# Two attention blocks on one core: the layer-1 score convolution moved behind the projection and split in halves twice

## The chip, the cores and the metric

The kernel runs on one core of one Trainium2 chip. The metric is the device time of one execution in microseconds (us), the lower the better. A core has TensorE (matrix products, PE in the profile), VectorE (DVE), ScalarE (ACT), GpSimd (POOL) and SyncE (SP, which here issues DMAs). Everything is computed in 32-bit floating point.

## The reference, cut to what matters

The input is `x` with 8 images of 512 channels and 32 x 32 = 1024 positions. Two layers follow each other. Both normalise in groups of channels, make queries, keys and values by a 512 x 512 product over the channels, apply attention over the 1024 positions, project, and add the input.

```python
# layer 0: 32 groups, 8 heads of 64 channels
h = group_norm(x, gn_weight, gn_bias)
q, k, v = split(einsum('oc,bct->bot', w_qkv, h) + b_qkv)
weight = softmax(einsum('bct,bcs->bts', q * scale, k * scale))
a = einsum('bts,bcs->bct', weight, v)
x = x + einsum('oc,bct->bot', w_proj, a) + b_proj
# layer 1: 8 groups, one head of 512 channels
xn = group_norm(x, gamma, beta)
q, k, v = conv1x1(xn, q_w, q_b), conv1x1(xn, k_w, k_b), conv1x1(xn, v_w, v_b)
attn = softmax(einsum('bqc,bck->bqk', q, k) * scale)
x = x + conv1x1(einsum('bqk,bkc->bqc', attn, v), p_w, p_b)
```

## The kernel before, in words

**Fused weights.** In layer 1 the query and key weights are multiplied into one matrix `m` in the prologue, and value and output weights into `z`. So layer 1 needs one convolution `g` (with `m`), the scores of `g` against `h`, a product `z` by token, and the weighted sum of `z`.

**Products by halves (`wino`).** A 512-wide product is split in halves on both sides and computed with 7 half-size products in place of 8, in the scheme of Strassen and Winograd. It needs sums and differences of the halves of both factors ("factors"): `left_sums` and `right_sums` list them as steps, and `image_factors` and `weight_factors` hold them. The weights' factors are made once and kept in DRAM (`keep`). `wino` runs the products in the order 1, four in `middle`, then 4 and 3. One product is a step: 4 matmuls of 128x512 (two output halves `i`, two slices `k` of the sum). Its results pass through three pairs of accumulator banks, a, b and c. ScalarE copies bank a (`t`), VectorE adds (`u`, `w`, and the outputs in `done`). The last two steps (4 and 3) are put on `tail` and issued inside the next product, after its step 1, so that TensorE has other work while the banks are read.

**Halves twice (`conv2`).** The convolutions k and q of layer 0, from the second image on, apply the scheme twice: 49 matmuls of 128x256 in four "pairs" of outer products. The inner factors of the image are made on GpSimd (`inner_factors`), those of the weights in the prologue (`keep2`, GpSimd), and the weights come in two parts.

**Background and hooks.** `background` is a list of small pieces of VectorE or GpSimd work; each step of a product issues a few of them (`back`). `all_background` issues what is left. `hooks` are calls after given steps of a product. What is issued with `keep_in_program_order` keeps its place in its engine's queue; the rest is ordered by a scheduler when the program is built. All TensorE work is kept in program order.

**The order of one image b** (b from 1): attention of layer 0 (`attention0`), g of layer 1 for image b-1 with the projection p of image b begun in its tail, p with the residual and the group-norm statistics (`projection`), layer 1's scores for b-1 in two parts (`scores1`), z, the weighted sum (`values1`), then v of image b+1 and its k and q. So layer 1 lags one image behind. For image 0 there is no layer 1 yet: v of image 1, then p, then k and q. After the last image layer 1 of the last image runs alone.

**Attention of layer 0.** Eight blocks, four pairs of heads `hp` by two halves of the positions `tb`. In each, 8 pairs of score matmuls, ScalarE's exponentials, VectorE's 7 additions into `sum`, 8 pairs of `av` matmuls, the `sums` matmuls with ones, VectorE's reciprocal, and a trip through DRAM (`rows`, then `r`) which spreads the reciprocals over the partitions; GpSimd (for the last block VectorE, `scaled`) multiplies `a` by `r`. `extra` lists pieces of work after the score matmuls and after the av matmuls of each block.

**Group norm.** `half_stats` and `end_stats` are VectorE's bn_stats and aggregate. `group_mean` is a small matmul `gmean` over the channels, and VectorE's copy, `d`, `d2`, `dv`. `affine` is the matmul `gvar` on `dv`, and scale and offset. In the kernel before, `norm_hooks` places the flush of the background, gmean and gvar in part 0 of the scores, after its third, fourth and fifth step.

**Weights** are loaded by `load_weight` in the order of `uses` into three buffers.

Of the kernel before, what the change touches and what calls it, by code (L numbers as in the profile page):

```python
# [29 lines left out]
def two_attention_blocks_kernel(  # L30
# [145 lines left out]
    def main_path(ctx):  # L176
# [117 lines left out]
        wdram2 = {n: dram.tile([P, 7, 7, P], F32, name=f"sums2_{n}") for n in "qk"}  # L294

        def keep2(n, t):

            u = wpool.tile([P, 4, 7, P], F32, tag="w", name=f"prepare2_{n}")
            quarter = lambda k, i: t[:, :, k, ts(i, P)]
            a11, a21, a12, a22 = quarter(0, 0), quarter(0, 1), quarter(1, 0), quarter(1, 1)  # L300
            s1, s2, s3, s4 = (u[:, i, :, :] for i in range(4))
            for dst, x, y, op in (
                (s1, a21, a22, ALU.add), (s2, s1, a11, ALU.subtract), (s3, a11, a21, ALU.subtract),
                (s4, a12, s2, ALU.subtract),
            ):
                nc.gpsimd.tensor_tensor(dst, x, y, op)
            for j, f in enumerate((a11, a12, s4, a22, s1, s2, s3)):
                nc.sync.dma_start(wdram2[n][:, :, j, :], f)

        twice = [("k", 0), ("k", 1), ("q", 0), ("q", 1)]  # L310
        uses = ["v", "p", *twice] if B > 1 else ["p"]
        for b in range(1, B):
            uses += ["m", "p", "z"] + (["v", *twice] if b + 1 < B else [])
# [3 lines left out]
        def load_weight():  # L317
            if uses:
                n = uses.pop(0)
                t = wpool.tile([P, 7 * C], F32, tag="w", name=f"w_{n[0]}_{len(uses)}")  # L320
                if n in twice:
                    t = t.rearrange("p (i j m) -> p i j m", i=4, j=7)
                    i = n[1]
                    t = t[:, : 4 - i]
                    nc.sync.dma_start(t, wdram2[n[0]][:, 4 * i : 4 + 3 * i])
                else:
                    t = t.rearrange("p (i k m) -> p i k m", i=7, k=2)
                    nc.sync.dma_start(t, wdram[n])
                loaded.append((n, t))
# [10 lines left out]
        def image_factors(h, uid):  # L340

            tiles = [pair_tile(f"t{i}_{uid}") for i in (1, 2, 4)]
            halves = lambda t: (t[:, :HT], t[:, HT:])
            return right_sums(
                [halves(t) for t in h[:2]], [halves(t) for t in h[2:]],
                [lambda j, t=t: t[:, j, :] for t in tiles], nc.vector.tensor_sub,
            )
# [52 lines left out]
        def inner_factors(hf, uid):  # L400

            f, steps = {}, []
            for p in ORDER:
                t = big_tile(f"inner{p}_{uid}", (P, 4, 2 * P))
                t1, t2, t3, t4 = (t[:, i, :] for i in range(4))
                b11, b12, b21, b22 = (hf[p][k][:, ts(i, 2 * P)] for k in range(2) for i in range(2))
                f[p] = {1: b11, 2: b21, 3: b22, 4: t4, 5: t1, 6: t2, 7: t3}

                def make(ops=((t1, b12, b11), (t2, b22, t1), (t3, b22, b12), (t4, b21, t2))):
                    for dst, x, y in ops:  # L410
                        nc.gpsimd.tensor_tensor(dst, x, y, ALU.subtract)

                steps.append(make)
            return f, steps

        def conv2(n, f, bias, name, hooks=(), late=None):
# [123 lines left out]
            last = [lambda: biased_half(0, 1), lambda: biased_half(1, 0)]  # L540
# [3 lines left out]
            pair(3, (3, 4), [(0, 1), (1, 0)], [(0, 1), (1, 0)], [load_weight, *last])  # L544
# [3 lines left out]
        def reciprocals(total, uid, across):  # L548
# [14 lines left out]
            nc.sync.dma_start(rows.rearrange("j i n -> i j n"), rc[0:P:32, :, :])  # L563
            if across:
                r = pair_tile(f"r_{uid}")
                for j in range(2):
                    row = rows[j : j + 1].rearrange("j i n -> j (i n)")
                    nc.sync.dma_start(r[:, j, :], row.to_broadcast([P, HT]))
            else:
                r = rpool.tile([P, HT], F32, tag="r", name=f"r_{uid}")  # L570
                for j in range(2):
                    row = rows[j : j + 1].rearrange("j i n -> j (i n)")
                    nc.sync.dma_start(r[ts(j, 64), :], row.to_broadcast([64, HT]))
# [3 lines left out]
        def attention0(b, q, k, v, extra):  # L577
            a = channel_tiles(f"a0_{b}")
            n = 0
            for hp in range(KC):  # L580
                for tb in range(2):
# [31 lines left out]
                    r = reciprocals(total, uid, False)  # L613
                    if (hp, tb) != (KC - 1, 1):
                        nc.gpsimd.tensor_tensor(dst, dst, r, ALU.mult)  # L615
                    else:
                        scaled = lambda dst=dst, r=r: nc.vector.tensor_mul(dst, dst, r)

            assert not extra
            return a, scaled  # L620


        def scores1(b, gf, hf, uid, hooks):
# [7 lines left out]
            def part(j):  # L631
# [34 lines left out]
                wino(f"sc_{uid}_{j}", mm, done, middle=(6, 2, 5, 7) if j else (2, 5, 6, 7), hooks=() if j else hooks)  # L666
# [85 lines left out]
        def prologue():  # L752
# [35 lines left out]
            k = conv(weight_factors(first["k"][0]), hf, pcols("bk0"), "k0_0")  # L788
            finish()
            keep2("k", first["k"][0])  # L790
            norm1.group_mean(acc_tile("gmean_0_1")[:, :KC])
# [6 lines left out]
            for n in "pmz":  # L798
                t, steps = prepare(n)
                later.append(steps)  # L800
                later.append([lambda n=n, t=t: keep(n, t), load_weight])
# [3 lines left out]
                lambda: tc.keep_in_program_order(nc.vector.tensor_add(obias[0], bias[2], pcols("bp0"))),  # L805
            ])
# [27 lines left out]
        def attention_steps(a, scaled, b):  # L834
            af, steps = image_factors(a, f"a_{b}")
            return af, [[], [scaled, lambda: background.extend(steps)]]

        def projection(b, af, xt):

            norm = GroupNorm(1, f"1_{b}")  # L840

            def residual(i, r, c, ps, u):
                oc = 2 * r + i
                xh = xt[oc][:, ts(c, HT)]
                nc.vector.scalar_tensor_tensor(xh, ps, obias[0][:, oc : oc + 1], xh, ALU.add, ALU.add)
                if u is not None:
                    nc.vector.tensor_add(xh, xh, u)  # L847
                background.append(lambda: norm.half_stats(oc, c, xh))

                if c == 1 - r:  # L850
                    background.append(lambda: norm.end_stats(oc))
# [6 lines left out]
            by_channel(weight("p"), af, f"p_{b}", residual, after=[load_weight, store])  # L858
            return norm

        def norm_hooks(norm, uid):
            return [
                [], [], [all_background], [lambda: norm.group_mean(acc_tile(f"gmean_{uid}")[:, :KC])],
# [3 lines left out]
        def values(b, h, hooks=()):  # L867

            hf, steps = image_factors(h, f"h0_{b}")
            background.extend(steps)  # L870
# [21 lines left out]
        def layer1_scores(b, h, hooks):  # L892
            hf, steps = image_factors(h, f"h1_{b}")
            background.extend(steps)
            g = conv(
                weight("m"), hf, ubias, f"g1_{b}", middle=(2, 5, 6, 7), hooks=hooks, back=4,
                after=[load_weight, lambda: background.extend(gsteps)],
            )
# [6 lines left out]
            return hf, gf  # L905

        def layer1_rest(b, hf, gf, hooks, ahead):
            e, total, ef = scores1(b, gf, hf, f"1_{b}", hooks)
# [19 lines left out]
        for b in range(B):  # L928
# [11 lines left out]
            for i, f in enumerate(applies):  # L940
                extra[2 * i + 3].append(f)
            if b > 0:
                extra[0] += late
            psum_pools(f"attention_{b}", 1)
            a, scaled = attention0(b, q, k, v, extra)
            psum_pools(f"products_{b}", 2)
            xt = [load_x(b, c, "x") for c in range(KC)]
            af, ends = attention_steps(a, scaled, b)
            if b > 0:
                hf, gf = layer1_scores(b - 1, h, ends)  # L950
                norm1 = projection(b, af, xt)
# [5 lines left out]
                layer1_rest(b - 1, hf, gf, norm_hooks(norm1, f"1_{b}"), ahead)  # L957
                if b + 1 < B:
                    v, f, norm0 = values(b + 1, h)
                    q, k, late = keys_and_queries(b + 1, f, norm0, ())  # L960
            elif B > 1:
                v, f, norm0 = values(1, h, ends)
                norm1 = projection(0, af, xt)
                q, k, late = keys_and_queries(1, f, norm0, norm_hooks(norm1, "1_0")[1:])
            else:
                for f in sum(ends, []):
                    f()
                all_background()
                norm1 = projection(0, af, xt)
                finish()  # L970
                for f in sum(norm_hooks(norm1, "1_0"), []):
# [4 lines left out]
        hf, gf = layer1_scores(B - 1, h, ())  # L976
        layer1_rest(B - 1, hf, gf, (), ())
# [196 lines left out]
```

## Time and profile before

| what | value |
|---|---|
| time, median of 3 runs | 2902.52 us (2901.96 to 2906.08) |
| span of the profiled execution | 2900.9 us |
| TensorE busy | 2886.5 us, 10838 matmuls |
| VectorE busy | 1932.5 us, 2613 instructions |
| ScalarE busy | 872.2 us, 1117 instructions |
| GpSimd busy | 468.9 us, 525 instructions |
| DMA | 267.97 MB, mean 92 GB/s |
| start of the attention of images 1, 2, 3 | 330.10, 685.26, 1040.78 us |

A line of the timeline gives the start, the duration, the engine, the line of the kernel, the operation, what it writes and what it reads, the shape, how many instructions the line joins, and in brackets how long the engine was idle before and what ended that. TensorE's records count two for one matmul in 32-bit: "x8" is four matmuls. Nearly all matmuls are recorded at line 67, a helper, so they are told apart by the names of their tiles: `psa_g` is bank a of product g, `psb_sc` bank b of the scores. A line of the waits gives the total, the number of times and the longest. One period of the image loop, from attention to attention, is about 355.2 us.

### The profile page before, as it was taken

To read this page: it belongs to the slowest core of one execution; us is meant where nothing else is said; L and a number is where in the kernel's file an instruction comes from. 1 tells how busy PE (TensorE), PEld (TensorE's weight loads), DVE (VectorE), ACT (ScalarE), POOL (GpSimd) and SP (SyncE) were. 2 spreads that over 40 slices of the span, in tenths; PEclk is the share of its full clock that TensorE was granted. 3 is DMA by queue.
4 is the path that set the end of the run, shared out by engine and by line. 5 is a ranking of instruction groups with operands and counts; after the bars stand their busy time and mean duration, and the time that the engine had idled before them with its cause. 6 is when DMAs were issued, how large, how long until landed. Compare 5 with 4: busy or idle time off the path is not lost.

```text
span 2900.9 us, 29024 instructions
## 1 busy us (share of the span) xinstructions
PE 2886.5 (100%) x10838; PEld 1500.3 (52%) x10838; DVE 1932.5 (67%) x2613; ACT 872.2 (30%) x1117; POOL 468.9 (16%) x525
## 2 busy tenths in 40 slices
PE   9999999999999999999999999999999999999999
PEld 5435634565345653457434574346733458334544
DVE  5488687567766578665776557866577665776555
ACT  1251451214512055121551115411163112631110
POOL 3023210032200321003210122102121031110000
PEclk9999999999999999999999999999999999999999
DMA  8433403123122231222212232122411224011201
GB/s 277 153 137 109 159 19 110 72 103 132 34 98 92 95 113 48 84 92 105 107 48 80 92 135 77 48 80 99 154 55 44 80 103 151 26 59 65 94 1 66
DMA packets 84186, 267.97 MB, mean 92 GB/s; under 512 B 10371, under 2 KB 29891, under 8 KB 75974
## 3 DMA queue, kind: packets, MB, share of 16 engines
q1 hardware_dynamic: 83622, 265.89, 25.5%
q8 instruction: 87, 1.43, 0.2%
q14 instruction: 61, 0.50, 0.1%
q10 hardware_dynamic: 416, 0.16, 0.0%
HBM read 216.30 MB, written 49.72 MB: 92 GB/s over the span
## 4 chain that ended last, share of the span: by engine, by line
PE 98%; issue 1%; DVE 0%; POOL 0%; ACT 0%; DVEq 0%; POOLq 0%
PE sc L67 16%; PE av L67 15%; PE psb_sc L67 6%; PE psb_av L67 6%; PE psa_av L67 4%; PE psa_sc L67 4%; PE psc_av L67 4%; PE psc_sc L67 4%; PE psb_g L67 3%; PE psb_z L67 3%; PE psb_p L67 3%; PE psb_v L67 3%; PE psb_k L67 3%; PE psb_q L67 2%; PE psa_g L67 2%; PE psa_v L67 2%
## 5 line engine op out<-in xcount | busy, mean ns | idle before, releaser
L598 DVE TENSOR_TENSOR sum<-sum,e 128x1024 f32<-128x1024 f32 x384 | 518.6, 1351 | 40.4 <-DVE sum L598 0.5
L594 ACT ACTIVATE e<-sc 128x1024 f32<-128x1024 f32 x512 | 476.8, 1052 | 72.9 <-PE sc L67 72.9
L67 PE MATMUL sc<-q,k 64*128 64x512 f32 x2048 | 458.3, 596 | 0.0
L67 PE MATMUL av<-e,v 128*64 128x512 f32 x2048 | 453.6, 595 | 0.0
L67 PEld LDWEIGHTS sc<-q,k 64*128 64x128 f32 x2048 | 192.3, 186 | 239.3 <-ACT e L594 110.3
L67 PEld LDWEIGHTS av<-e,v 128*64 128x64 f32 x2048 | 141.4, 137 | 304.3 <-issue 302.3
L561 POOL TENSOR_TENSOR all_recs<-all_recs,rc 128x256 f32<-128x256 f32 x72 | 64.4, 894 | 880.2 <-DVE rc L559 880.2
L559 DVE RECIPROCAL rc<-sums 128x256 f32<-128x256 f32 x72 | 126.4, 1756 | 89.7 <-PE sums L67 87.4
L615 POOL TENSOR_TENSOR a<-a,r 128x512 f32<-128x512 f32 x56 | 109.5, 1955 | 274.0 <-DMA r<-rows 247.5
L646 ACT ACTIVATE e<-e 128x512 f32<-128x512 f32 x96 | 60.5, 630 | 232.7 <-DVE e L645 232.7
L612 ACT COPY a<-av 128x512 f32<-128x512 f32 x64 | 37.4, 585 | 305.2 <-PE av L67 305.2
L596 DVE TENSOR_TENSOR sum<-e,e 128x1024 f32<-128x1024 f32 x64 | 78.6, 1228 | 59.8 <-ACT e L594 59.8
L67 PE MATMUL psa_sc<-g,h 128*128 128x512 f32 x256 | 115.7, 594 | 0.0
L67 PE MATMUL psa_av<-e,z 128*128 128x512 f32 x256 | 113.3, 595 | 0.0
L128 POOL TENSOR_TENSOR rstd<-ve,mhalf 128x4 f32<-128x4 f32 x16 | 16.7, 1043 | 499.9 <-DVE ve L126 499.9
L140 ACT ACTIVATE h<-h,b,s 128x1024 f32<-128x1024 f32 x62 | 78.5, 1270 | 60.7 <-DMA h<-in_x 48.0
L67 PEld LDWEIGHTS psa_sc<-g,h 128*128 128x128 f32 x256 | 48.1, 190 | 57.9 <-issue 56.2
L67 PEld LDWEIGHTS psa_av<-e,z 128*128 128x128 f32 x256 | 48.0, 190 | 57.3 <-issue 55.4
L67 PE MATMUL psb_k<-inner_h,w_k 128*128 128x256 f32 x294 | 75.4, 383 | 0.0
L67 PE MATMUL psb_q<-inner_h,w_q 128*128 128x256 f32 x294 | 74.9, 383 | 0.0
L249 ACT COPY t_sc<-psa_sc 128x512 f32<-128x512 f32 x32 | 18.7, 585 | 181.7 <-DVE x L847 152.4
L444 POOL TENSOR_TENSOR k<-k,k 128x256 f32<-128x256 f32 x28 | 20.0, 727 | 291.0 <-DVE u_k L439 291.0
(304 smaller groups left out, 4580.8 us busy)
## 6 DMA issues: line engine op xcount, KB each, us to landing
x<-in_x SPq DMA_DIRECT2D x36, 512.0 KB
h<-in_x SPq DMA_DIRECT2D x32, 512.0 KB
r<-rows SPq DMA_DIRECT2D x128, 128.0 KB
spill<-x SPq DMA_DIRECT2D x32, 512.0 KB
h<-spill SPq DMA_DIRECT2D x32, 512.0 KB
x<-spill SPq DMA_DIRECT2D x32, 512.0 KB
out<-x SPq DMA_DIRECT2D x64, 256.0 KB
w_p<-sums_p SPq DMA_DIRECT2D x8, 1792.0 KB
```

The costliest lines, as they stand in the source:

```text
L67: tc.keep_in_program_order(nc.tensor.matmul(*args, **kw))
L140: tc.keep_in_program_order(nc.scalar.activation(dst, src, AF.Identity, bias=b, scale=s))
L249: nc.scalar.copy(t1[i], ps["a", i])
L444: nc.gpsimd.tensor_tensor(d, x, y, ALU.add)
L559: nc.vector.reciprocal(rc, sums)
L561: nc.gpsimd.tensor_tensor(all_recs, all_recs, rc, ALU.add)
L594: nc.scalar.activation(e, sc, AF.Exp, scale=(C // 8) ** -0.5)
L596: nc.vector.tensor_add(total, es[0], e)
L598: nc.vector.tensor_add(total, total, e)
L612: nc.scalar.copy(dst, av)
L615: nc.gpsimd.tensor_tensor(dst, dst, r, ALU.mult)
L646: nc.scalar.activation(dst, dst, AF.Exp, scale=scale)
```

## The change

It does four things.

1. **g by halves twice.** For all images but the last, g is computed by `conv2` in place of `conv`. The weight factors of `m` for both levels are made in the prologue, beside the k convolution, and `m` is loaded in two parts.
2. **p before g.** The projection comes right after the attention, and g after it. GpSimd makes g's inner factors while p runs.
3. **Factors spread over the attention.** The differences of `h` (for g) and of `a` (for p), which were made in one go at the attention's end and during g, are placed in the attention's blocks. For this the last pair of heads takes its two halves in the order 1, 0. The last block's `rows` and `r` transfers are issued by ScalarE.
4. **Statistics later.** The bn_stats of p are gathered in a list and given to the background in part 0 of the scores; the flush, gmean and gvar stand in part 1, after its third, fourth and fifth step. Some additions of p are kept in program order, and p's middle steps run 5, 6, 7, 2.

The core of the diff:

```diff
-        wdram2 = {... for n in "qk"}
+        wdram2 = {... for n in "qkm"}
...
-            uses += ["m", "p", "z"] + (["v", *twice] if b + 1 < B else [])
+            uses += ["p", *twice["m"], "z"] + (["v", *twice["k"], *twice["q"]] if b + 1 < B else [])
...
-            last = [lambda: biased_half(0, 1), lambda: biased_half(1, 0)]
+            last = [lambda: biased_half(1, 0), lambda: biased_half(0, 1)]
...
-                for tb in range(2):
+                for tb in (0, 1) if hp < KC - 1 else (1, 0):
...
-                    r = reciprocals(total, uid, False)
-                    if (hp, tb) != (KC - 1, 1):
+                    last = (hp, tb) == (KC - 1, 0)
+                    r = reciprocals(total, uid, False, nc.scalar if last else nc.sync)
+                    if not last:
...
-                background.append(lambda: norm.half_stats(oc, c, xh))
+                stats.append(lambda: norm.half_stats(oc, c, xh))
...
             return [
-                [], [], [all_background], [lambda: norm.group_mean(acc_tile(f"gmean_{uid}")[:, :KC])],
+                [], [all_background], [lambda: norm.group_mean(acc_tile(f"gmean_{uid}")[:, :KC])],
                 [lambda: norm.affine(acc_tile(f"gvar_{uid}")[:, :KC])],
             ]
...
-            g = conv(
-                weight("m"), hf, ubias, f"g1_{b}", middle=(2, 5, 6, 7), hooks=hooks, back=4,
-                after=[load_weight, lambda: background.extend(gsteps)],
-            )
+            after = [lambda: background.extend(gsteps)]
+            if inner:
+                g = conv2("m", inner, ubias, f"g1_{b}", after=after)
+            else:
+                g = conv(weight("m"), hf, ubias, f"g1_{b}", middle=(2, 5, 6, 7), back=4, after=[load_weight, *after])
...
+                hf, t = image_factors(h, f"h1_{b - 1}")
                 extra[0] += late
+                for i, fs in enumerate((t[:1], t[1:2], (t[2], t[4]), (t[6], t[3]), (t[5], t[7]), steps[:2], steps[2:4])):
+                    extra[2 * i + 3] += fs
...
-                hf, gf = layer1_scores(b - 1, h, ends)
-                norm1 = projection(b, af, xt)
+                inner, sums2 = inner_factors(hf, f"h1_{b - 1}", tc.keep_in_program_order)
+                for f in sums2:
+                    f()
+                norm1, stats = projection(b, af, xt, [scaled, steps[7]])
+                gf = layer1_scores(b - 1, hf, inner)
...
-                layer1_rest(b - 1, hf, gf, norm_hooks(norm1, f"1_{b}"), ahead)
+                hooks = [[], [], [lambda: background.extend(stats)]], [[], *norm_hooks(norm1, f"1_{b}")]
+                layer1_rest(b - 1, hf, gf, hooks, ahead)
```

## The prediction

> **What bounds the kernel now.** I read the page first (busy shares and the chain that ended last), then the view of TensorE's waits, then the timelines of TensorE and VectorE over one image period, since a share of 100 % doesn't say how much of it is work.
>
> ```profile
> PE 2886.5 (100%) x10838; PEld 1500.3 (52%) x10838; DVE 1932.5 (67%) x2613; ACT 872.2 (30%) x1117; POOL 468.9 (16%) x525
> ...
> PE 98%; issue 1%; DVE 0%; POOL 0%; ACT 0%; DVEq 0%; POOLq 0%
> ```
>
> The reader sees that TensorE is the chain itself: 98 % of the path to the end. No other engine is above 67 %.
>
> ```profile
> PE tr_wk L70 <- DMA rawk<-in_w: 4.0, 2, 3.8
> PE psa_v L67 <- POOL h L142: 0.8, 1, 0.8
> ```
>
> These are the largest waits of TensorE in the whole run (total, times, longest), and both are in the prologue; all its listed waits come to about 7 us of 2901. So time can only be won by fewer or shorter matmuls, and anything that makes TensorE wait is added in full. The question is what the new order does to the waits.
>
> The place I use most is the end of the scores of layer 1. TensorE first, then VectorE over the same stretch and 10 us further:
>
> ```profile
> 861.46 3.60 PE L67 MATMUL psb_sc<-sg,t_h 128*128 128x512 f32 x8
> 864.90 0.28 PE L67 MATMUL gmean<-mv,gm 128*128 128x4 f32 x2
> 865.04 3.68 PE L67 MATMUL psb_sc<-g,h 128*128 128x512 f32 x8
> 868.55 0.28 PE L67 MATMUL gvar<-dv,gm 128*128 128x4 f32 x2
> ```
> ```profile
> 865.17 0.69 DVE L238 TENSOR_TENSOR u_sc<-psb_sc,t_sc 128x512 f32<-128x512 f32 x1 [1.02 <-PE psb_sc L67]
> ...
> 866.35 0.16 DVE L121 TENSOR_TENSOR dv<-d,mv 128x4 f32<-128x4 f32 x1
> 867.04 0.69 DVE L238 TENSOR_TENSOR w_sc<-psb_sc,t_sc 128x512 f32<-128x512 f32 x1 [0.52 <-PE psb_sc L67]
> ...
> 877.75 1.22 DVE L652 TENSOR_TENSOR sum<-sum,e 128x1024 f32<-128x1024 f32 x1
> 878.88 0.68 DVE L645 TENSOR_TENSOR e<-psc_sc,u_sc 128x512 f32<-128x512 f32 x1
> ```
>
> Today the two small group-norm matmuls sit in part 0 of the scores: gmean is issued, VectorE makes dv at 866.35, before the next w_sc, and gvar at 868.55 finds it ready. Steps before and after follow at 3.43 us. VectorE is idle before these ops there. Ten microseconds later it is not: from 877.13 on one op follows the other without a gap.
>
> ```profile
> 704.54 8.76 DVE L598 TENSOR_TENSOR sum<-sum,e 128x1024 f32<-128x1024 f32 x6
> 714.86 1.76 DVE L559 RECIPROCAL rc<-sums 128x256 f32<-128x256 f32 x1 [1.55 <-PE sums L67]
> ```
>
> In an attention block the six sum adds end at 713.31 and the sums matmul starts near 714.15: 0.8 us of slack in a block of 14.65 us.
>
> **What the Trainium skill says.** "TensorE: Matmul & The Clock Gate" (Part 3, what overlaps and what doesn't) has matmuls in strict order, and its first table gives the other compute engines strict queues. The trace agrees: what follows gmean and gvar never overtakes them. So a group-norm matmul whose input is late holds all work behind it. "SBUF — State Buffer" (SBUF: two separate sides) says that a VectorE op with two SBUF inputs and a GpSimd op lock each other out. The trace agrees: the low_recs op at 806.37 took 0.94 us beside GpSimd's all_recs, against 0.42 at 702.00. "DMA: Bandwidth & Descriptors" (Issuing engines are not separate DMA queues) says the issuing engine changes little but the issuing; no run so far shows r issued from ScalarE.
>
> **The change, part by part.**
>
> *g by halves twice (7 of the 8 images; the last keeps the old form).* The old g has 28 matmuls of 128x512. One step of four takes 3.433 us on the timeline, so 28 x 0.858 = 24.03 us. The stretch with g and p mixed runs from 802.65 to 854.60: 51.95 us for 15 steps, 15 x 3.433 = 51.50, so 0.45 us is lost there, at the steps where w_g queues behind VectorE's factors of a (from 811.68 to 817.70). The new g has 49 matmuls of 128x256. The k and q convolutions show their price: 634.44 to 685.19 is 50.75 us, less 6.95 for two v steps and 0.28 for the norm matmuls is 43.52 us for 98; spacing in undisturbed pairs 0.4315, so 42.29 of work and about 0.6 us of stalls for each. New g: 49 x 0.4315 + 0.6 = 21.74. Gain 24.03 + 0.45 - 21.74 = 2.74 us an image, 19.2 us in seven.
>
> *Inner factors on GpSimd.* 28 subtractions an image at 0.83 us (mean of the same op for k and q) are 23.3 us. They start about 3.4 us after the attention's last av matmul and end near 27. g starts at 24.6 and takes its first two products then, which have long been made. Hidden by p. Slower VectorE ops beside them hit only the x additions, which no matmul of p waits for.
>
> *p first, factors of a spread.* p runs alone: its steps begin 0.6, 4.0, 7.5, 10.9, 14.3 us after the last av matmul. Today r takes 5.8 us from the reciprocal's end (805.92) to its use (811.68). The new issue waits on ScalarE for the reciprocal and for rows to land; queued behind it are the t_p copies, and u_p waits for these at about 9.4; ScalarE is free again near 5. The scaled a comes at 8 to 10, its first user is product 2 at 14.3. No wait.
>
> *h and a factors in the attention.* One or two subtractions a block, 0.6 us each. Blocks with one before the last add fit in the slack of 0.8. In the built order block 4 (counting from 0) has two before its last add: about +1.0, so sums waits some 0.3 us once per image.
>
> *End of g.* Its tail runs before the scores, and the bias activations on ScalarE (0.67 each) come ahead of the t_sc copy: I give 0.3 us.
>
> *Statistics moved into part 1 of the scores.* This decides. bn_stats now enter the background after part 0's third step, part 1 runs its products 1, 6, 2, 5, 7; a flush of the background stands after 2, gmean after 5, gvar after 7. In the built order of VectorE, from the u_sc of step 6's second half: bn_stats, aggregate, bn_stats, aggregate, two t1, sum, t2, sum, t2, sum, two e differences, two t4, gmean copy, w_sc, d, w_sc, d2, e, dv. With the trace's spacings (512-wide ops 0.60, 1024-wide 1.13, bn_stats to aggregate 0.72, small ones 0.12 to 0.19), and step 6 starting at S: u_sc at S + 3.71 (865.17 - 861.46), t1 at 5.99, the sums at 7.19, 8.92 and 10.65, gmean copy at 14.18, second w_sc at 15.1, dv from 16.5 to 16.65. TensorE reaches gvar after four steps and gmean: S + 4 x 3.433 + 0.14 = S + 13.87. So gvar waits about 2.8 us, with z's first step and everything else queued behind it. Lower end: even with no backlog, dv stands behind the second w_sc, which needs the last matmul ahead of gvar: 13.73 + 0.27 + 0.60 + 0.19 + 0.60 + 0.16 = 15.6, so at least 1.7. Upper end: GpSimd's first sum copy (1.6 us) late by as much, 4. I take 2.83, 19.8 us in seven.
>
> *The rest.* One weight load more per image (m in two parts, 3.2 MB for 1.8 MB) is hidden by the three weight buffers and 92 GB/s mean traffic. Prologue: four more GpSimd sums of 2.1 us and four VectorE ones, beside k and z products that bound it; image 0 has v, p, k, q as before. Together 0, give or take 1 us.
>
> *Sum:* per image -2.74 + 2.83 + 0.3 + 0.3 = +0.69; times 7 = +4.8; 2902.5 + 4.8 = 2907.3 us.
>
> **The rivals.**
> A: VectorE keeps up and dv is ready. For: it is only 67 % busy. Against: dv behind w_sc in its queue. Time 2902.5 - 7 x (2.74 - 0.6) = 2887.5, faster.
> A': only the floor of the wait, 1.7: 2902.5 - 7 x (2.74 - 0.6 - 1.7) = 2899.4, no measurable change.
> B: more waits than counted, for instance r from ScalarE's queue coming late for product 2, or VectorE's residual ops of p held up by GpSimd's 23 us beside them, 1.2 us more an image: 2907.3 + 8.4 = 2915.7, slower. For: the lock seen above. Against: 4 us of slack for r.
>
> **How the numbers follow.** Main case (2903 to 2912) 0.45, of it 0.25 within 0.2 % (up to 2908.3) and 0.2 above; A' 0.2, within; A 0.15, faster; B 0.2, slower. Faster 0.15, same 0.25 + 0.2 = 0.45, slower 0.2 + 0.2 = 0.40. Range 2891 to 2916: it leaves out most of A and the upper end of B.
>
> **What would show it.** In the profile after: g rows of 128x256, spaced 0.43; a stretch of g near 21.7 us; a wait of TensorE for dv at gvar, near 2.8 us in each of seven images, as the longest kind in the view of waits; small waits of sums for sum; an image period of about 355.9 against 355.2. If gvar waits less than 1 us, the step on the statistics is wrong, and the time falls below 2893. If TensorE waits for a or u_p in p, B holds.

## The result and the profile after

The changed kernel took 2926.01 us (median of 4 runs, 2923.62 to 2929.73), the kernel before 2904.3 us in the same comparison. The ratio is 1.0076, with a 95 % interval of 1.0059 to 1.0094: slower by 22 us, and 10 us beyond the upper end of the range.

The page's busy line and the largest rows of the view of TensorE's waits (total, times, longest):

```profile
PE 2884.6 (99%) x11132; PEld 1560.2 (53%) x11132; DVE 2002.9 (69%) x2753; ACT 924.3 (32%) x1201; POOL 688.9 (24%) x781
```
```profile
PE gvar L67 <- DVE dv L121: 15.6, 7, 2.2
PE ps_wz L67 <- issue: 4.4, 1, 4.4
PE tr_wk L70 <- DMA rawk<-in_w: 3.6, 1, 3.6
PE psb_v L67 <- DVE u_v L238: 2.5, 1, 2.5
```

The first row is the wait that the prediction named: seven times, one per image, for dv. The second (0.5 us in the kernel before) and the fourth weren't foreseen; both lie outside the image loop. These three rows together are 22.5 us, but the cheaper g should have paid for most of that. So the waits alone don't explain the loss. (The page's chain of after was followed back over 13 % of the span only, so it isn't read here.)

I cut both traces at the stages' first matmuls:

| stage | before, us | after, us | difference |
|---|---|---|---|
| start to first attention (prologue) | 120.23 | 127.06 | +6.83 |
| attention of image 0 | 117.23 | 117.89 | +0.66 |
| image 0 between the attentions (v, p, k, q) | 92.56 | 95.43 | +2.87 |
| attention, images 1 to 7, each | 117.45 | 117.66 | +0.21 |
| p and g to z's end, images 1 to 7 | 114.04 in five, 114.39, 114.21 | 116.27 in four, 114.59 in three | +10.0 in all |
| the rest | | | 0 |

That is 21.8 us, the whole difference of the two spans (2900.9 and 2922.6). The fifth row has two values after, 1.7 us apart, at one and the same wait. This is image 1, then image 2, on TensorE's timeline:

```profile
548.07 0.39 PE L67 MATMUL gvar<-dv,gm 128*128 128x4 f32 x2 [2.23 <-DVE dv L121]
548.32 5.39 PE L67 MATMUL psa_z<-w_z,h 128*128 128x256 f32 x16
```
```profile
905.67 0.39 PE L67 MATMUL gvar<-dv,gm 128*128 128x4 f32 x2 [2.23 <-DVE dv L121]
905.92 3.27 PE L67 MATMUL psa_z<-w_z,h 128*128 128x256 f32 x14
```

Behind the same wait of 2.23 us, 16 records of z take 5.39 us in image 1 and 3.70 in image 2 (where the window cuts the second line off after 14). The view of the windows gives, after the length of each window, TensorE's busy time and, ahead of the last two numbers, the granted clock (PEclk). For image 1:

```profile
545.81:549.22 3.41, 1.18 (x7) 1.07 (x7) 2.88 (x10) 1.20 (x2) 0.45 (x1) 1.00 0.00 0
549.22:552.63 3.41, 3.41 (x9) 2.68 (x9) 0.00 (x0) 0.65 (x2) 1.18 (x4) 0.50 0.00 0
```

and for image 2:

```profile
900.79:904.21 3.42, 2.66 (x7) 0.87 (x5) 3.42 (x9) 0.00 (x0) 0.00 (x0) 1.00 0.00 0
904.21:907.62 3.41, 1.95 (x10) 1.77 (x11) 2.08 (x7) 1.26 (x2) 1.17 (x2) 1.00 0.00 0
907.62:911.03 3.41, 3.41 (x14) 2.37 (x13) 0.00 (x0) 1.17 (x2) 0.46 (x3) 1.00 0.00 0
```

Behind the first wait the clock was 0.50 for 3.41 us; behind the other it stayed at 1.00. A wait of TensorE here costs its length, and at times a stretch of 3.41 us at half the clock as well, which loses half of it: the 1.7 us by which the two values differ. What tells the two kinds of wait apart is in the last section.

The theory that the experiments test: (1) gvar's wait costs 2.4 us in each image and, in four of them, 1.7 us of half clock; (2) the prologue's loss is a VectorE delay made by GpSimd, and (3) so is that of image 0. The rivals: VectorE's backlog as such, a late load of the p weights, and too many pinned subtractions (pinned: kept in program order).

### The profile page after: what moved, and what is told of

Same layout as the page of the kernel before. It is cut to its first block, busy times and chain, and to the rows that moved or that the text cites. A ratio compares the mean times of both kernels' runs of the same rounds, so it can differ in the third digit from the quotient of the medians.

```text
span 2922.6 us, 30278 instructions
## 1 busy us (share of the span) xinstructions
PE 2884.6 (99%) x11132; PEld 1560.2 (53%) x11132; DVE 2002.9 (69%) x2753; ACT 924.3 (32%) x1201; POOL 688.9 (24%) x781
## 5 line engine op out<-in xcount | busy, mean ns | idle before, releaser
L411 POOL TENSOR_TENSOR inner_h<-h,inner_h 128x256 f32<-128x256 f32 x112 | 96.4, 863 | 2.7
L411 POOL TENSOR_TENSOR inner_h<-h 128x256 f32<-128x256 f32 x56 | 57.2, 1022 | 151.3 <-PE psc_av L67 151.3
L652 POOL COPY sum<-e 128x1024 f32<-128x1024 f32 x8 | 8.8, 1102 | 283.6 <-ACT e L648 283.6
```

Source lines behind the costliest of these rows:

```text
L411: pin(nc.gpsimd.tensor_tensor(dst, x, y, ALU.subtract))
```

## The experiments

Each time is set against that of the kernel before on the same chip (2902.5 us for items 1, 2, 4 and the first kernel of item 3, 2902.6 us for the others). Where a stage is named, its time is taken from the trace as in the table.

**1. Group norm's matmuls moved on into z.**

```diff
-                hooks = ..., [[], *norm_hooks(norm1, f"1_{b}")]
+                hooks = ..., [[], [], [all_background]]
...
-                weight("z"), hf, f"z1_{b}", hooks=[[], [], [], [], [sums]], back=3,
+                weight("z"), hf, f"z1_{b}", hooks=[*zhooks, [sums]], back=3,
...
+            zhooks = [
+                [lambda: norm.group_mean(acc_tile(f"gmean_{uid}")[:, :KC])], [],
+                [lambda: norm.affine(acc_tile(f"gvar_{uid}")[:, :KC])], [],
+            ]
```

In the order of issue gmean stands after z's first step and gvar after its third, one step later than the expectation says.

> The changed kernel with gmean moved behind z's first step and gvar behind z's second, nothing else. Theory: TensorE's wait for dv (2.4 us of lost spacing in each of 7 images) and the half-clock stretch behind it (1.7 us in 4 of them) are the whole price of the late statistics: 7 x 2.4 + 4 x 1.7 = 23.6 us, so about 2902 us (2899 to 2906), no wait at gvar, and a mean granted clock back near 0.998. Rival: VectorE's backlog of statistics and score sums is the limit and shows up at the next use (z's banks or the sums matmul): 2912 to 2926 us.

Measured: 2903.81 us, ratio to before 1.0002 (0.9993 to 1.0011). gvar is gone from the waits, and all seven images take 112.09 us from p to z's end. So moving two small matmuls takes away the loss of the loop (2.5 us in three images, 4.2 in four), and in the loop no other wait takes its place. The backlog of VectorE is real, but nothing in this stage needs its result so soon.

**2. Is the clock a price of its own?** Eight matmuls of 128x128 whose result isn't used are put ahead of each gvar.

```diff
+        def warm(uid):
+            ps = acc_tile(f"warm_{uid}")
+            for i in range(8):
+                matmul(ps[:, :P], ones, ones, start=True, stop=True)
...
+                hooks[1][-1].insert(0, lambda: warm(b))
```

> The changed kernel with eight extra 128x128 matmuls (about 1.7 us, result unused) ahead of each gvar, so that TensorE is idle for about 0.6 us instead of 2.4; dv comes no earlier. Theory: four of seven images lose a further 1.7 us because an idle TensorE is granted half the clock for a stretch; with the gap filled all seven take the short form (114.6 us from p to z's end), mean clock near 0.998, and about 2919 us, although more matmuls run. Rival: dv is later in those four images: 2926 us, and the long images stay.

Measured: 2920.48 us, mean clock 0.998, and all seven images take 114.58 or 114.59 us.

```profile
543.85 3.68 PE L67 MATMUL psb_sc<-g,h 128*128 128x512 f32 x8
547.37 1.95 PE L67 MATMUL warm<-ones 128*128 128x128 f32 x16
549.76 0.39 PE L67 MATMUL gvar<-dv,gm 128*128 128x4 f32 x2 [0.44 <-DVE dv L121]
550.00 3.70 PE L67 MATMUL psa_z<-w_z,h 128*128 128x256 f32 x16
```

gvar starts 5.91 us after the last scores step begins, with or without the extra matmuls (5.90 before: 548.07 - 542.17), so dv came no earlier. But the step behind it takes 3.70 us in every image. In the other profiles with this loop, those of item 3's two kernels and of item 4, four, five and four of the seven images were long. The median fell by 5.5 us and not by 6.8; outside the loop, where nothing was changed, this profile differs from that of the changed kernel (prologue to 124.96, image 0's stage 99.23 us). Work for nothing made the kernel faster: the half clock is a loss of its own, 4 x 1.69 = 6.8 us here.

**3. The prologue: who holds VectorE?** On the changed kernel's timelines, first TensorE, then VectorE, then GpSimd:

```profile
100.72 1.64 PE L70 MATMUL tr_wv<-ident,rawv 128*128 128x128 f32 x13 [0.34 <-DVE k L387]
106.74 2.04 PE L67 MATMUL ps_wz<-rawp,natv 128*128 128x512 f32 x2 [4.39 <-issue]
```
```profile
100.58 0.15 DVE L115 COPY gmean<-gmean 128x4 f32<-128x4 f32 x1
100.76 1.22 DVE L117 TENSOR_TENSOR d<-mv,gmean 128x4 f32<-128x4 f32 x1
102.01 2.00 DVE L119 TENSOR_TENSOR d<-d 128x4 f32<-128x4 f32 x1
104.05 2.00 DVE L121 TENSOR_TENSOR dv<-d,mv 128x4 f32<-128x4 f32 x1
105.96 1.27 DVE L718 COPY natv<-tr_wv 128x512 f32<-128x512 f32 x2
```
```profile
97.72 8.31 POOL L306 TENSOR_TENSOR prepare_m<-prepare_m 128x896 f32<-128x896 f32 x4 [9.98 <-DVE prepare_m L286]
```

Three operations on 4 elements, 0.16 us each in the kernel before, take 1.22, 2.00 and 2.00 us: they end at 101.98, 104.01 and 106.04, each within 0.02 us of the end of one of GpSimd's four sums for m (101.96, 104.00, 106.02). Behind them in VectorE's queue wait the copies of the transposed v weights, and ps_wz waits for these. The view calls it "issue", since no semaphore event names the cause. The rival is a late load: the p weights are requested from 89.04 on, where it was 82.92.

The first kernel moves gmean into the z product, so that the copies come first:

```diff
-            norm1.group_mean(acc_tile("gmean_0_1")[:, :KC])
...
-            product(wv, raw_p, "z")
+            product(wv, raw_p, "z", {7: lambda: norm1.group_mean(acc_tile("gmean_0_1")[:, :KC])})
```

> The changed kernel with the prologue's gmean of image 1 issued inside the z product, so that VectorE copies the transposed v weights before it comes to d, d2 and dv; GpSimd's four sums for m stay where they are. Theory: the three tiny VectorE ops, held by GpSimd's 2.1 us ops, delay those copies, and the stall of 4.4 us starts a half-clock stretch: the wait at ps_wz falls under 1 us, the product takes 14 us again, the first attention starts 6.8 us earlier, total about 2919 us. Rival: the p weights, loaded later behind the m transfers, are what ps_wz waits for: the wait stays near 4 us and the time near 2926.

Measured: 2922.16 us. ps_wz waits 0.5 us, as in the kernel before, and the first attention starts at 120.62. The load isn't the cause. The median fell by 3.9 us and not by 6.8; in this profile image 0's stage took 99.27 us, against 95.43 in that of the changed kernel (item 4).

The second leaves the order and cuts GpSimd's operations:

```diff
-                tc.keep_in_program_order(nc.gpsimd.tensor_tensor(dst, x, y, op))
+                for i in range(4 if n == "m" else 1):
+                    part = ...
+                    tc.keep_in_program_order(nc.gpsimd.tensor_tensor(part(dst), part(x), part(y), op))
```

(`part` takes 2, 2, 2 and 1 of the 7 slices in turn.)

> The changed kernel with each of GpSimd's four sums for m in the prologue cut into four (2, 2, 2 and 1 of 7 slices), same total work, everything else as it is. Theory: a VectorE op with two inputs in SBUF waits for one whole GpSimd op; with ops of about 0.6 us in place of 2.1 us the three tiny ops d, d2 and dv end after about 2 us and not 5.3, the copies of the v weights follow, and ps_wz waits about 1 to 2 us (4.4 before). Rival: VectorE is held as long as GpSimd has work queued, whatever its pieces: the wait stays at 4 us or more.

Measured: 2923.05 us in a single run, first attention at 120.33. VectorE, then GpSimd:

```profile
100.67 0.16 DVE L117 TENSOR_TENSOR d<-mv,gmean 128x4 f32<-128x4 f32 x1
100.87 0.59 DVE L119 TENSOR_TENSOR d<-d 128x4 f32<-128x4 f32 x1
101.50 0.38 DVE L121 TENSOR_TENSOR dv<-d,mv 128x4 f32<-128x4 f32 x1
101.97 1.29 DVE L722 COPY natv<-tr_wv 128x512 f32<-128x512 f32 x2
```
```profile
98.25 8.53 POOL L310 TENSOR_TENSOR prepare_m<-prepare_m 128x256 f32<-128x256 f32 x14 [0.63 <-DVE prepare_m L286]
```

GpSimd is busy throughout as before, yet the three operations end 4.2 us earlier, and the copies run at full speed beside it: they have one input, in PSUM. So in this stage the length of a single GpSimd operation held VectorE, and not the GpSimd work in its queue. ps_wz waits 0.5 us. "SBUF — State Buffer" of the Trainium skill (SBUF: two separate sides) states an exclusive lock: of a VectorE operation with two SBUF inputs and a GpSimd operation that reads SBUF, the one that starts first holds the shared ports for its whole instruction, and the other blocks. The three ends in the changed kernel, each within 0.02 us of a GpSimd operation's end, agree; item 4 shows a case that this doesn't cover. The prediction cited the lock and applied it to p alone.

**4. Image 0: a factors beside GpSimd's.** The changed kernel issues four pinned subtractions for a in the middle of v. This kernel spreads them over more steps:

```diff
-                v, f, norm0 = values(1, hf, [[], steps[:4], steps[4:7], [scaled, steps[7]]])
+                v, f, norm0 = values(1, hf, [[], steps[:2], steps[2:4], steps[4:6], [steps[6], scaled, steps[7]]])
```

> The changed kernel with image 0's a factors spread over four steps of v instead of three (two or three subtractions at a time, not four). Theory: the wait of psb_v for u_v (2.5 us) comes from four pinned subtractions ahead of u_v, each about 1.1 us beside GpSimd's factors; with two ahead it vanishes: about 2923 us. Rival: any pinned pair beside GpSimd is late enough: wait over 1 us, 2925 to 2926.

Measured: 2926.4 us, no gain; the wait is 3.6 us. In this kernel's timeline of VectorE:

```profile
257.53 5.62 DVE L960 TENSOR_TENSOR t_a<-a 128x512 f32<-128x512 f32 x2
263.07 0.68 DVE L238 TENSOR_TENSOR u_v<-psb_v,t_v 128x512 f32<-128x512 f32 x1
```

Two subtractions took 5.62 us, where such a pair takes 1.28. GpSimd's inner factors run at 0.7 us each up to 261.46, one close behind the other, and the first subtraction ends only at 262.01, during the last of them. In the profile of the changed kernel the two engines alternated and four subtractions took 4.5 us; in this one and in those of items 1 to 3 VectorE stood still. With four subtractions the wait was then 4.8 to 4.9 us, with two 3.6. So the count is worth about 1.2 us, two subtractions at 0.60; the rest is the standstill, and my theory was wrong. In the profile of item 1 the wait of 4.85 also brought the half clock: the 8 records behind it took 3.62 us, where the 8 before it took 1.89.

**5. All three out.** Item 1 and the first kernel of item 3 together, and image 0's subtractions after v's last hook, when GpSimd's factors are done. The line that is new here:

```diff
-                v, f, norm0 = values(1, hf, [[], steps[:4], steps[4:7], [scaled, steps[7]]])
+                v, f, norm0 = values(1, hf, [[], [], [], [], [*steps[:7], scaled, steps[7]]])
```

> The changed kernel with group norm's matmuls moved into z, the prologue's gmean moved into the z product, and image 0's a factors all placed after v's last hook, when GpSimd's factors are done. Theory: each loss is local to its stage, so they add: first attention at 120.6 us (127.1), image 0's stage after the attention near 92.6 us (95.4 to 99.3), p to z's end near 112.1 us per image; together about 2889 us, which is 13 below the kernel before. Rival: image 0's p now waits for its a factors and gives back 3 us or more: 2892 to 2897 us.

Measured: 2890.89 us, ratio to before 0.9957 (0.994 to 0.9973). The stages: 120.03, 92.56 and 112.09 us. The losses add, and p of image 0 doesn't wait for its factors. The subtractions now follow each other at 0.60 us, as two starts of pairs 1.20 us apart show:

```profile
257.83 1.28 DVE L965 TENSOR_TENSOR t_a<-a 128x512 f32<-128x512 f32 x2
259.03 1.29 DVE L965 TENSOR_TENSOR t_a<-a,t_a 128x512 f32<-128x512 f32 x2
260.24 1.29 DVE L965 TENSOR_TENSOR a<-a,a 128x512 f32<-128x512 f32 x2
```

**6. What is g by halves twice worth?** The same kernel with g as before:

```diff
-            uses += ["p", *twice["m"], "z"] + (["v", *twice["k"], *twice["q"]] if b + 1 < B else [])
+            uses += ["p", "m", "z"] + (["v", *twice["k"], *twice["q"]] if b + 1 < B else [])
...
-                inner, sums2 = inner_factors(hf, f"h1_{b - 1}", tc.keep_in_program_order)
-                for f in sums2:
-                    f()
+                inner = None
```

> The same three waits out, but g computed by halves once, as in the kernel before (28 matmuls of 128x512, no inner factors on GpSimd, m loaded whole). Theory: g by halves twice is worth 24.0 - 21.7 = 2.3 to 2.8 us in each of 7 images, so this one is 16 to 20 us slower than the kernel with the three waits out: 2905 to 2909 us, and p to z's end near 114.5 us. Rival: the gain comes from the new order (factors out of g's way), not from fewer columns: at most 8 us slower.

Measured: 2904.43 us, ratio 1.0002 (0.9993 to 1.0011), 114.04 us from p to z's end. The halves are worth 1.95 us an image, 13.5 us in all, less than I expected. Here the new order with g as before gives the 114.04 us that five of seven images had in the kernel before: in this stage, order and spreading bring nothing more by themselves than the 0.35 and 0.17 us of the other two.

**7. The attention's 0.2 us.** The kernel of item 5 with the differences of h pinned behind the sum adds:

```diff
-                hf, t = image_factors(h, f"h1_{b - 1}")
+                hf, t = image_factors(h, f"h1_{b - 1}", lambda *t: tc.keep_in_program_order(nc.vector.tensor_sub(*t)))
```

(and the same for image 0.)

> The three waits out, and the differences of h kept in program order, which puts them behind the last sum add of their attention block. Theory: the 0.2 us by which the attentions grew (0.65 in image 0) comes from two differences ahead of a last add: the attention takes 117.45 us again (117.66), so 8 images give about 2 us: 2887 us. Rival: the steps then hold up the next block's reciprocal instead: no gain, 2889 us or more.

Measured: 2888.65 us, ratio to before 0.995 (0.9933 to 0.9966): the fastest kernel of this study, 14 us below the one before. The attentions take 117.45 us again, 117.23 in image 0. Its largest waits of TensorE are the prologue's old ones:

```profile
PE tr_wk L70 <- DMA rawk<-in_w: 3.9, 1, 3.9
PE psa_v L67 <- POOL h L142: 0.8, 1, 0.8
```

## Why the prediction was wrong

The main mechanism was right, in place and cause: gvar waits for dv, seven times, and eats what g gains. VectorE's order and times came out nearly as added up. This is its end in image 1:

```profile
544.65 1.28 DVE L173 TENSOR_TENSOR t<-e,t 128x512 f32<-128x512 f32 x2
545.86 0.15 DVE L115 COPY gmean<-gmean 128x4 f32<-128x4 f32 x1
545.93 0.68 DVE L238 TENSOR_TENSOR w_sc<-psb_sc,t_sc 128x512 f32<-128x512 f32 x1
546.53 0.15 DVE L117 TENSOR_TENSOR d<-mv,gmean 128x4 f32<-128x4 f32 x1
546.60 0.68 DVE L238 TENSOR_TENSOR w_sc<-psb_sc,t_sc 128x512 f32<-128x512 f32 x1
547.20 0.15 DVE L119 TENSOR_TENSOR d<-d 128x4 f32<-128x4 f32 x1
547.27 0.68 DVE L647 TENSOR_TENSOR e<-psc_sc,w_sc 128x512 f32<-128x512 f32 x1
547.87 0.15 DVE L121 TENSOR_TENSOR dv<-d,mv 128x4 f32<-128x4 f32 x1
```

Step 6's second u_sc started at 535.43, so S is 531.72, and dv starts at S + 16.15; S + 16.5 was predicted. For an image without the half clock the sum works: +0.69 predicted, 0.55 + 0.21 = +0.76 measured. In part that is luck: the wait came out 0.3 us shorter than predicted and the gain of g 0.5 us smaller, and the two errors offset each other.

| step of the prediction | predicted, us | measured, us |
|---|---|---|
| gvar's wait, each image | +2.83 | +2.5 (114.59 - 112.09) |
| half clock behind it | not in the sum | +1.7 in four images |
| g by halves twice, with the end of g, each image | -2.74 + 0.3 | -1.95 |
| sums behind two subtractions, images 1 to 7 | +0.3 | +0.21 |
| p first, r from ScalarE's queue, seven images | no wait | no wait |
| "the rest": prologue and image 0 | 0, give or take 1 | +10.4 in the profile (6.83 + 0.66 + 2.87) |

The step that failed is "the rest", put at 0, give or take 1, where +10.4 us were measured. It named the four GpSimd sums, said they lie "beside k and z products that bound it", and stopped there. It checked TensorE and forgot that VectorE, in between, has to make the operands of the next TensorE product while GpSimd runs 2.1 us operations. The same lock was quoted in the prediction, with the trace's own 0.94 against 0.42 us, but used for p's additions only. Image 0 was put down "as before", though the diff gives it pinned subtractions among GpSimd's factors.

The second miss is a missing term. A wait was priced at its own length, and half the clock was in no case. 6.8 us behind gvar came from it. In the prologue the granted clock was 0.50 from 105.49 to 112.31, and the z product took 16.73 us where it was 13.97; so of the prologue's 6.83 us, 3.9 are the longer wait and 2.8 the clock. Of the 16.9 us between the predicted sum (+4.8) and the profile (+21.7), "the rest" and the half clock behind gvar account for all but a few tenths.

One size was off: the 0.45 us of lost time in the old g. I took it from the stretch after 802.65. That image takes 114.39 us, and five of seven take 114.04: it was an exception. The remaining 0.15 us of the gap between -2.44 and -1.95 is in the scores' start and the stalls in g: by the trace, p and g together now take 46.0 us to the scores' first matmul (504.06 - 458.04), 45.2 of it the matmuls' own spacing.

Of the rivals, A was out, as its "against" said. B (2915.7) had the right sign, but from waits in p that never came; the time was lost elsewhere.

## What to carry to other kernels

When TensorE is the bound, price a new wait as its length plus, where the trace shows it, a stretch at half clock (1.7 us each here), and go through every stage that the change touches, the prologue and first image too: a small operation that makes an operand is as much on the path as a matmul. Beside GpSimd operations, put VectorE's operations with two SBUF inputs behind those that TensorE waits for, or after the GpSimd work; cutting long GpSimd operations helped in the prologue, but beside a row of short ones in image 0 a subtraction still stood still. A small matmul that depends on a long chain can be worth issuing one stage later; here that cost nothing and was worth 22 us.

## What the runs showed of the hardware that was not expected

- The same idle time of TensorE (2.23 us in the view of the waits) was followed by half clock in four images and not in three, and the place of the wait tells which. The clock's records in the trace of the changed kernel show the half-clock stretches of these four images from 549.22, 1262.61, 1975.99 and 2334.39 on. They are 209, 209 and 105 times 3.4133 us apart, so they begin on a fixed grid of slots of that length. The rows of the windows above are such slots: in image 1 all of the 2.23 us falls into one, and in image 2 the edge at 904.21 cuts it into 0.76 and 1.46. In the four profiles that keep this wait (the changed kernel, both kernels of item 3, item 4) it occurs 28 times: 17 waits had 1.78 us or more in one slot, and half clock followed each of them; 11 had at most 1.70 us in one slot, and it followed none. That is no sharp limit, since elsewhere in these traces up to 1.8 us without a matmul in a slot was not followed by half clock. "TensorE: Matmul & The Clock Gate" (HAM oscillation, and What's actually happening) of the Trainium skill puts the throttle after an idle window of about 3.4 us, free-running: the length of the slots agrees, but here a slot that was idle for about half its length was enough. Item 2 fits: its extra matmuls leave 0.44 us, and half clock followed in none of the seven images.
- A VectorE subtraction beside back-to-back GpSimd subtractions stood still for more than 4 us in five profiles and took turns with them in another, in the same stage. What decides between the two stays open. Image 0's stage took 95.4 us in the profile where they took turns, and 98.2 to 99.4 us in those with the standstill.
